# Graph layer with neighbour quantiles: the last pair's upper tiles sorted batch by batch

## The chip, the cores and the metric

One core of a Trainium2 chip runs the whole kernel. The metric is the time of one execution on the device in microseconds (us), and less is better.

## What is computed

For each of 16 batches there are N = 1024 nodes with C = 64 features and a symmetric 0/1 adjacency. Features are normalised and passed through a relu, edges are dropped by a rule on ranks, and each node takes three weighted quantiles over the neighbours that are left, feature by feature. A two-layer network and the residual follow. The reference, cut:

```
h = relu(layernorm(x))
nb   = number of neighbours;  skip = (nb + 1) // 2 where nb > 10, else 1
rem  = neighbour & (skip > 1) & (rank % skip == skip - 1);  rem |= rem.T
nd   = (adjacency or self) without rem
s    = sort of h over the neighbours in nd, feature by feature
agg  = sum over (0.25, 0.25), (0.5, 0.5), (0.75, 0.25) of w * (s[lo] + frac * (s[hi] - s[lo]))
y    = relu((h + agg) @ W1 + b1) @ W2 + b2          # 64 -> 128 -> 64
out  = x + y * mask
```

The adjacency has a density of about 1/128, so a node has some 8 neighbours before edges are dropped.

## The kernel before

**Pairs and tiles.** The batches go in eight pairs (m = 0 to 7). For each batch `prepare` reads the adjacency, drops edges, ranks what is left and writes lists of neighbours (`idx`, L1116). Nodes are put in order of their number of neighbours and cut into 8 tiles of 128. Tiles share buffers by class, `CLASSES = (((0,), 13), ((1, 2, 3), 11), ((4, 5), 9), ((6, 7), 7))`: buffer g0 holds tile 0 with 13 slots, g1 tiles 1 to 3, g4 tiles 4 and 5, g6 tiles 6 and 7. Tiles 0 to 3 are the lower half, 4 to 7 the upper. A slot holds one neighbour's 64 features for both batches of the pair.

**Gathers.** An indirect DMA on POOL's queue (`fetch`, L1250) brings 128 rows of 64 features into one slot. A pair takes 126 of them, in the order of the classes, and in each class first all slots of the pair's first batch and then all of its second; the upper classes take 30 and 18.

**Sorting.** `aggregate` (L1329) runs a network of minima and maxima on DVE over the slots of a buffer (`sort`, L1270; operations L1285, L1288, L1289), multiplies the sorted rows by weights (L1296), and PE adds them into `acc` (L1298, with a 128x128 identity in float32). A tiny DVE write, `pause` (L1268), is what PE waits for. Some nodes with many neighbours keep slots in another tile's buffer as guests: ACT copies them across (L1352), and only then may DVE overwrite their old place (L1355). `terms` splits `acc` into three bf16 parts in `o` (ACT L1312, PE L1314). A half works on both batches at once, so its instructions are twice as wide as one batch needs. In the last pair (batches 14 and 15) the lower half goes first, then the upper.

**Back to node order.** `mlp` multiplies `o` by one-hot matrices `at_p` (L1373) to bring the rows back to node order: 8 matmuls `high` (L1392) and 8 `low` (L1397) for each half of a batch's nodes, one of each for every tile. ACT copies both out (L1404, L1406), two float32 products with W1 follow (L1410, L1411), a relu (L1414), the second layer (L1424, L1428), the mask `mask2` (L1432), the residual (L1433), and a DMA of the batch to `out` (L1419).

**Rows apart.** The 32 nodes of a batch with most neighbours are sorted elsewhere, in groups of eight batches (`gg`, `aggregate_group`). Their finished rows are put into `out` by an indirect DMA on POOL's queue (`scatter`, L1498, two for a group), after the batch's own rows: `mask2` zeroes their contribution there. The last group holds batches 8 to 15, so it is scattered at the end of the program. After that come the flag that tells whether a node had too many neighbours (`worst`, L1593, L1594), its load by all engines (L1686), and a branch (L1687) over a dense version that is not taken here.

**What sets the order.** `arrange` collects the whole program and puts the instructions of every engine in a fixed order, with a cost per instruction that it reckons itself (`Step.cost`). An engine then works through its list in that order; an instruction that has to wait holds up all behind it.

Of the kernel before, what the change touches and what calls it, by code (L numbers as in the profile page):

```python
# [600 lines left out]
class Step:  # L601
# [11 lines left out]
    def cost(self):  # L613
        sides = self.writes + self.reads
        most = max([u.count for u in sides] or [1])
        if self.engine == "PE":
            n, lines = self.writes[0].count, self.writes[0].lines
            if any(u.size == 4 for u in self.reads):
                busy = 223 if n <= 64 else max(428, n / 0.6)
            else:  # L620
                busy = max(25, n / 2.4 + 3)
# [127 lines left out]
def list_layer(  # L749
# [262 lines left out]
    def order(b):  # L1012
# [30 lines left out]
        nc.vector.scalar_tensor_tensor(mask2[:, b], place_f, float(FEW), mask[:, b], OP.is_ge, OP.mult)  # L1043
# [227 lines left out]
    def sort(lines, plan, first, coef, acc):  # L1271

        size = lines.shape[2]
# [19 lines left out]
        for n in taken:  # L1293
            now, ends = ends[:n], ends[n:]
            v = at(now[0], now[1] - now[0] if n > 1 else 0, n).rearrange("p s (k c) -> p s k c", c=C)
# [33 lines left out]
    def aggregate(m, o):  # L1329


        last = m == pairs - 1
        coef = coefs[m]
        for half in (0, 1) if last else (1, 0):
            acc = psum.tile([P, 4, 2, C], F32, name="acc", tag="agg", bufs=2)
            parts = CLASSES[2 * half:2 * half + 2][::1 if last else -1]
            for tiles, slots in parts:
                lo, n = tiles[0], len(tiles)
                nc.tensor.matmul(
                    acc[:, lo - 4 * half:lo - 4 * half + n], ident32, gathered[m, tiles][:, slots - 1],  # L1340
                    start=((tiles, slots) == parts[0]), stop=False, skip_group_check=True,
                )
            line = {}
            for tiles, slots in parts:
                for k in tiles:
                    for s, slot in enumerate(PLANS[slots][1]):
                        line[k, s] = gathered[m, tiles][:, slot, k - tiles[0]]
                        if s >= FULL[k] and (k, s) not in HOSTS:
                            nc.vector.memset(line[k, s], BIG)
            for host, guest, first, stop in GUESTS:  # L1350
                if host in line:
                    nc.scalar.copy(line[guest][first:stop], line[host][first:stop])  # L1352
            for host, lo, hi in BARE:
                if host in line:
                    nc.vector.memset(line[host][lo:hi], BIG)  # L1355
            for tiles, slots in parts:
                lo, n = tiles[0], len(tiles)
                g = gathered.pop((m, tiles))
                plan = PLANS[slots]
                yield from sort(  # L1360
                    g.rearrange("p s n h c -> p s (n h c)"), plan, window(tiles, slots)[0],
                    lambda s, many: coef[:, s:s + many, lo:lo + n].rearrange("p s n h -> p s (n h)"),
                    acc[:, lo - 4 * half:lo - 4 * half + n],
                )
            if half and not last:
                fetch(m + 1, CLASSES[2:])
            terms(acc, [o[:, 4 * half:4 * half + 4, :, C * n:C * n + C] for n in range(3)])
# [14 lines left out]
    def mlp(b, o):  # L1382

        res = wk.tile([P, NT, C], F32, name="y")
        nc.sync.dma_start(out=res, in_=x[b].rearrange("(t p) c -> p t c", p=P))
        for n in range(2):
            if (b, n) not in placed:
                yield from one_hot(b, n)
            at = placed.pop((b, n))
            high = psum.tile([P, HALF], F32, name="high", tag="agg", bufs=2)  # L1390
            settle([
                nc.tensor.matmul(high, o[:, t, 0:2 * C], at[:, t], start=(t == 0), stop=(t == NT - 1))  # L1392
                for t in range(NT)
# [378 lines left out]
```

## Time and profile before

| | |
|---|---|
| median of 15 runs | 1582.53 us (1577.84 to 1585.58) |
| profiled execution | 1581.2 us |
| its span, from the first to the last instruction | 1579.5 us |
| mean granted TensorE clock in it | 0.851 |
| first gather, last upper gather on POOL | 273.57 us, 1516.84 us |
| span's end less the last DVE operation on `y` | 16.1 us |

The span is the length of the profiled execution as the trace shows it; 1.7 us of the execution lie outside. Times in the rows below count from the start of the span. A row of the timeline gives the start, the duration, the engine, the line, the operation, output and inputs, and in brackets how long the engine was idle before and what ended that. A row of the groups gives the count, the busy time and the mean duration in ns, then the idle time before. DVE, ACT, PE, POOL and SP are the five engines; a letter q behind one means its instruction queue, where waits and branches stand.

### The profile page before, as it was taken

How to read it: one execution, taken by the hardware profiler on the slowest of the kernel's cores; microseconds unless marked ns; L12 is line 12 of the kernel's file. 1: busy time of each engine (PE TensorE's matmuls, PEld its weight loads, DVE VectorE, ACT ScalarE, POOL GpSimd, SP SyncE). 2: the span in 40 equal slices, each digit the busy share in tenths (PEclk: the TensorE clock that was granted, in tenths of full speed). 3: DMA queues.
4: the chain of work that ended last, by engine and by line, in shares of the span. 5: the costliest groups of instructions: out<-in, count | busy, mean ns of one | idle time of the engine just before them, and what ended most of it. 6: DMA issues, size and time to landing. Idle time of an engine off the chain costs nothing.

```text
span 1579.5 us, 25586 instructions
## 1 busy us (share of the span) xinstructions
PE 1059.6 (67%) x8371; PEld 657.9 (42%) x8385; DVE 1192.8 (76%) x3723; ACT 915.5 (58%) x2496; POOL 1140.4 (72%) x1051
## 2 busy tenths in 40 slices
PE   6777867889878887888569745488768712602235
PEld 3445444555554454545345424354435402301122
DVE  4625499956997789879884898977988997697660
ACT  6998886987958694978276931856826200200001
POOL 3177776777777777777777777777777777777730
PEclk9989979999998999899689976899979955955568
DMA  6353442442523252325232422323211211211100
GB/s 208 113 164 93 116 110 64 113 126 60 156 57 112 59 144 63 105 60 145 50 83 67 125 64 46 85 73 65 77 26 26 50 27 25 54 25 23 21 11 18
DMA packets 128481, 122.71 MB, mean 78 GB/s; under 512 B 94514, under 2 KB 95026, under 8 KB 128338
## 3 DMA queue, kind: packets, MB, share of 16 engines
q1 hardware_dynamic: 94994, 86.77, 19.4%
q0 software_dynamic: 33344, 34.21, 10.9%
q8 instruction: 68, 1.11, 0.3%
q14 instruction: 75, 0.61, 0.1%
HBM read 110.10 MB, written 9.07 MB: 75 GB/s over the span
## 4 chain that ended last, share of the span: by engine, by line
POOL 30%; ACT 22%; DVE 15%; issue 13%; PE 13%; DMA 6%; POOLq 0%; DVEq 0%; SPq 0%; ACTq 0%
POOL g L1250 28%; PE codeP L1072 5%; DMA g<-gtab,idx 4%; DVE g L1288 4%; ACT dist L978 4%; ACT sg L891 3%; DVE g L1289 3%; ACT kept L1001 3%; ACT ne L911 3%; ACT waste L1170 2%; ACT waste L1165 1%; ACT xt L1178 1%; PE tp L898 1%; POOL gg L1455 1%; PE rk L968 1%
## 5 line engine op out<-in xcount | busy, mean ns | idle before, releaser
L1250 POOL DMA_INDIRECT g<-gtab,idx x1008 | 1092.5, 1084 | 359.1 <-issue 289.8
L1288 DVE TENSOR_TENSOR g<-g 128x512 f32<-128x512 f32 (+3 forms) x408 | 281.6, 704 | 43.6 <-DMA g<-gtab,idx 26.7
L1289 DVE TENSOR_TENSOR g<-g 128x512 f32<-128x512 f32 (+3 forms) x408 | 282.4, 705 | 10.7 <-DMA gg<-g 8.1
L1298 PE MATMUL acc<-g,kf 128*128 128x256 f32 (+2 forms) x448 | 142.3, 459 | 182.1 <-DVE pause L1268 109.2
L1072 PE MATMUL codeP<-pack,perm 128*128 128x332 bf16 x1024 | 182.2, 318 | 21.9 <-DVE perm L1047 21.4
L978 ACT ACTIVATE dist<-rk,bias 128x512 f16<-128x512 f32 x256 | 167.3, 701 | 25.1 <-DVE bias L953 11.8
L1298 PEld LDWEIGHTS acc<-g,kf 128*128 128x128 f32 x448 | 89.4, 231 | 208.7 <-DVE pause L1268 115.5
L968 PE MATMUL rk<-kb,cnt 128*128 128x512 bf16 x256 | 109.0, 426 | 73.4 <-ACT dist L978 67.3
L1001 ACT ACTIVATE kept<-kp 128x512 fp8e4<-128x512 f32 x248 | 149.3, 620 | 13.6 <-PE kp L996 11.8
L898 PE MATMUL tp<-kb,sg 128*128 128x128 bf16 x1024 | 106.3, 241 | 72.1 <-ACT sg L891 54.7
L911 ACT ACTIVATE ne<-tp 128x512 fp8e4<-128x512 f32 x248 | 138.8, 612 | 19.4 <-PE tp L904 10.9
L973 PEld LDWEIGHTS <-ne 128*128 128x128 fp8e4 x1024 | 87.2, 106 | 129.1 <-issue 104.4
L891 ACT ACTIVATE sg<-at 128x1024 bf16<-128x1024 f32 x121 | 127.0, 1081 | 3.9 <-DMA at<-in_adj_dram 3.8
L1072 PEld LDWEIGHTS <-perm 128*128 128x128 bf16 x1024 | 91.9, 100 | 86.0 <-DVE perm L1047 45.6
L898 PEld LDWEIGHTS <-sg 128*128 128x128 bf16 x1024 | 80.3, 109 | 94.0 <-ACT sg L891 63.0
L973 PE MATMUL rk<-kw,ne 128*128 128x128 fp8e5 x1024 | 114.3, 237 | 0.0
L979 DVE TENSOR_SCALAR rem<-dist,half 128x1024 bf16<-128x1024 f16 x128 | 64.7, 505 | 57.2 <-ACT dist L978 56.4
L996 PE MATMUL kp<-kw,rem 128*128 128x128 fp8e5 x1024 | 99.1, 218 | 0.0
L991 PE MATMUL kp<-ne,kw 128*128 128x512 fp8e4 x256 | 97.8, 382 | 0.1
L992 PE MATMUL kp<-rem,kw 128*128 128x512 bf16 x256 | 96.9, 379 | 0.0
L1373 DVE TENSOR_SCALAR at_p<-iota,node 128x512 bf16<-128x512 f16 x256 | 83.3, 373 | 7.0 <-PE low L1397 7.0
L1077 ACT CAST st<-codeP 128x4 bf16<-128x4 f32 x128 | 21.2, 165 | 113.5 <-PE codeP L1072 113.4
(178 smaller groups left out, 2052.9 us busy)
## 6 DMA issues: line engine op xcount, KB each, us to landing
at<-in_adj_dram SPq DMA_DIRECT2D x122, 512.0 KB
g<-gtab,idx POOLq DMA_INDIRECT x1008
xt<-in_x_dram SPq DMA_DIRECT2D x16, 256.0 KB
y<-in_x_dram SPq DMA_DIRECT2D x16, 256.0 KB
gtab<-xt SPq DMA_DIRECT2D x16, 256.0 KB
out_dram<-y SPq DMA_DIRECT2D x16, 256.0 KB
spare<-in_adj_dram SPq DMA_DIRECT2D x6, 512.0 KB
gg<-g SPq DMA_DIRECT2D x32, 48.0 KB
```

Source lines behind the costliest of these rows:

```text
L891: nc.scalar.activation(sg, at, AF.Sign)
L898: run.append(nc.tensor.matmul(tp[:, s], sg[:, m * P:(m + 1) * P], ident16, start=(s == 0), stop=(s == 3 and t // 4 != n), skip_group_check ...
L911: nc.scalar.activation(to, tp, AF.Relu, saturate=False)
L968: run = [nc.tensor.matmul(rk, cnt[:, ts], blocks[:, 4 * n:4 * n + 4, None].to_broadcast([P, 4, P]), start=True, stop=False, skip_group_che ...
L973: run.append(nc.tensor.matmul(rk[:, s * P:(s + 1) * P], ne[:, 4 * n + s, ts], upper, start=False, stop=(s == 3), skip_group_check=True,))
L978: nc.scalar.activation(dist[:, n * HALF:(n + 1) * HALF], rk, AF.Abs, bias=bias[:, t:t + 1])
L1001: nc.scalar.activation(kept[:, 4 * n:4 * n + 4], kp, AF.Relu, saturate=False)
L1072: run.append(nc.tensor.matmul(flat, perm[:, t, k * P:(k + 1) * P], pack[:, t], start=False, stop=(t == NT - 1), skip_group_check=True,))
L1250: return nc.gpsimd.indirect_dma_start(out=gathered[m, tiles][:, slot, k - lo, h], out_offset=None, in_=tables[2 * m + h][0], in_offset=bas ...
L1288: nc.vector.tensor_tensor(at(f, df, n), pa, pb, one)
L1289: ins = nc.vector.tensor_tensor(pa if back else pb, pa, pb, other)
L1298: nc.tensor.matmul(acc, ident32, lines[:, s], start=False, stop=(s == now[-1] and not ends), skip_group_check=True)
```

## The change

It has seven parts.

1. The planner's cost of a PE matmul on 4-byte data is `60 + n` for fewer than 512 columns, and 850 from there, where it was 223 up to 64 columns and then the larger of 428 and n/0.6. `arrange` then orders instructions differently in the whole program, from about row 437 of DVE's list on.
2. In the last pair the upper classes are fetched batch by batch: g4 and g6 of batch 14, then g4 and g6 of batch 15.
3. `aggregate` runs the last pair's upper half for batch 14 and then for batch 15, each with instructions half as wide.
4. Ahead of each of these two, `between` builds the batch's one-hot matrices and starts `high` and `low` with the lower four tiles (`sums`). Behind each, `mlp` adds only the upper four tiles.
5. In these two batches `low` is added to the copy of `high` by DVE (L1444), so that one product with W1 (L1448) is left of two; the product with the second bias is issued ahead; `out` is written in halves of 128 KB (L1468).
6. The rows apart of batches 14 and 15 are not scattered. `bring_back` picks them out of the group's sums with four small identity matmuls, two ACT copies, three ACT casts and two DVE subtractions (L1575), and writes them as bf16 parts into tile 0 of `o`; `mask2` of these batches is the plain mask. The last group's scatter is cut to 96 of its 128 rows and stands right behind `aggregate_group`.
7. `worst` and the flag are computed ahead of the last pair's results.

POOL's list, from the last pair's gathers of tiles 1 to 3 (g_16544) to the branch at the end; g_16715 is g4, g_16891 or g_16769 is g6. Before:

```order
L1250 DMA g_16544<-gtab,idx 128x64 x54
L1250 DMA g_16715<-gtab,idx 128x64 x30
L1250 DMA g_16891<-gtab,idx 128x64 x18
L1498 DMA out_dram<-gx,gto 16384x64 x2
L1686 TENSOR_LOAD flag
L1687 COMPARE_AND_BRANCH
```

Now:

```order
L1253 DMA g_16544<-gtab,idx 128x64 x54
L1253 DMA g_16715<-gtab,idx 128x64 x15
L1253 DMA g_16769<-gtab,idx 128x64 x9
L1253 DMA g_16715<-gtab,idx 128x64 x15
L1253 DMA g_16769<-gtab,idx 128x64 x9
L1580 DMA out_dram<-gx,gto 16384x64 x2
L1772 TENSOR_LOAD flag
L1773 COMPARE_AND_BRANCH
```

The 24 gathers of batch 14 now stand ahead of the 24 of batch 15. The scatters wait for the gathers ahead of them on the queue and for `out` of batches 12 and 13, no longer for batches 14 and 15.

DVE's list at the end of the program, from the last weighting of sorted rows (g6) to the flag. Before:

```order
L1296 TENSOR_TENSOR g6_16891<-g6_16891,coef_15426 128x3x256
L1268 MEMSET pause_127 128x1
L1432 TENSOR_TENSOR yp_17518<-yp_17518,mask2_120 128x256
L1433 TENSOR_TENSOR y_17489<-y_17489,yp_17518 128x256
L1432 TENSOR_TENSOR yp_17553<-yp_17553,mask2_120 128x256
L1433 TENSOR_TENSOR y_17489<-y_17489,yp_17553 128x256
L1432 TENSOR_TENSOR yp_17591<-yp_17591,mask2_120 128x256
L1433 TENSOR_TENSOR y_17562<-y_17562,yp_17591 128x256
L1432 TENSOR_TENSOR yp_17626<-yp_17626,mask2_120 128x256
L1433 TENSOR_TENSOR y_17562<-y_17562,yp_17626 128x256
```

Now:

```order
L1300 TENSOR_TENSOR g6_16769<-g6_16769,coef_15426 128x3x2x64 x2
L1271 MEMSET pause_127 128x1
L1444 TENSOR_TENSOR highs_17710<-highs_17710,low_17579 128x512
L1444 TENSOR_TENSOR highs_17726<-highs_17726,low_17589 128x512
L1491 TENSOR_TENSOR yp_17713<-yp_17713,mask2_120 128x256
L1492 TENSOR_TENSOR y_17692<-y_17692,yp_17713 128x256
L1491 TENSOR_TENSOR yp_17729<-yp_17729,mask2_120 128x256
L1492 TENSOR_TENSOR y_17692<-y_17692,yp_17729 128x256
```

Four rounds of mask and residual stood behind the last sorted row, one for each half of each batch; now two do, those of batch 15, and batch 14's stand among batch 15's sort.

ACT's list in the last pair, from the rows apart (`few`) to the last terms of batch 14's upper half (acc_17375; acc_17220 is the lower half). Copies from g4 to g6 are the guests, first those of batch 14 and then those of batch 15:

```order
L1569 COPY few_17367<-back_17362 32x128
L1570 COPY few_17367<-back_17362 16x128
L1364 COPY g6_16769<-g4_16715 64x64
L1364 COPY g6_16769<-g4_16715 32x64
L1316 CAST o_17019<-acc_17220 128x8x64 x2
L1573 CAST o_17019<-few_17367 32x2x64
L1364 COPY g6_16769<-g4_16715 64x64
L1316 CAST o_17019<-acc_17220 128x8x64
L1573 CAST o_17019<-few_17367 32x2x64 x2
L1364 COPY g6_16769<-g4_16715 32x64
L1316 CAST o_17019<-acc_17375 128x4x64 x3
```

Batch 15's first guest copy stands between the first and the second cast of `few`, and DVE's two subtractions on `few` stand between operations of batch 14's sort.

The diff, cut:

```
-                busy = 223 if n <= 64 else max(428, n / 0.6)
+                busy = 60 + n if n < 512 else 850
...
-    def aggregate(m, o):
+    def aggregate(m, o, between=None):
...
+            for sides in ((0, 1), (1, 2)) if last and half else ((0, 2),):
+                hs, one = slice(*sides), sides[0] if last and half else None
...
+                if one is not None:
+                    yield from between(one, False)
...
+                            line[k, s] = gathered[m, tiles][:, slot, k - tiles[0], hs]
...
+                    else:
+                        lines, weigh = g[:, :, :, one], partial(
+                            lambda s, many, lo, n, h: coef[:, s:s + many, lo:lo + n, h], lo=lo, n=n, h=one
+                        )
...
+                    for h in ((0, 1),) if m < pairs - 2 else ((0,), (1,)):
+                        fetch(m + 1, CLASSES[2:], halves=h)
...
+                if last and not half:
+                    bring_back(m, o)
+                if one is not None:
+                    yield from between(one, True)
...
+    def sums(o, at, n, some, tiles=None, late=False):
...
+        if begun:
+            begun = [sums(o, placed[b, n], n, range(NT // 2, NT), begun[n]) for n in range(2)]
...
+                nc.scalar.copy(highs, high)
+                nc.vector.tensor_tensor(highs, highs, low, OP.add)
+                run = bias(4, *(("misc", 1), ("agg", 2))[n])
+                hp = psum.tile([P, HALF], F32, name="hp", tag="code", bufs=2)
+                nc.tensor.matmul(hp, w1, highs, start=True, stop=True)
...
+    def bring_back(m, o):
...
+                run.append(nc.tensor.matmul(
+                    back[:SLICE + SLICE * q, q, h], ident32[:, lo - SLICE * q:lo + SLICE], sums[:, C * q:C * q + C],
+                    start=not run, stop=(len(run) == 3), skip_group_check=True,
+                ))
...
+        nc.scalar.copy(few, back[:, 1])
+        nc.scalar.copy(few[:SLICE], back[:SLICE, 0])
+        for n in range(3):
+            to = o[:FEW, 0, :, C * n:C * n + C]
+            nc.scalar.copy(to, few)
+            if n < 2:
+                nc.vector.tensor_tensor(few, few, to, OP.subtract)
...
+            def between(h, done):
+                b = 2 * m + h
+                if not done:
+                    for n in range(2):
+                        yield from one_hot(b, n, *((("at_p", 1), ("ne", 2)), (("ne", 2), ("wide", 1)))[h][n])
+                    begun[h] = [sums(o[:, :, h], placed[b, n], n, range(NT // 2), late=True) for n in range(2)]
+                else:
+                    yield from mlp(b, o[:, :, h], begun[h])
...
             yield from aggregate_group(grp - 1)
+            scatter(grp - 1, P - 2 * SLICE)
+            yield from aggregate(m, o, between)
...
-    for grp in range(B // GROUP):
-        if ("out", grp) in gathered:
-            scatter(grp)
```

207 lines of the change are left out of this document (122 added, 85 removed).

## The prediction

> **What bounds the kernel now.** I read the page's head first, then the shares of the chain that ended last, then POOL's timeline.
>
> ```profile
> PE 1059.6 (67%) x8371; PEld 657.9 (42%) x8385; DVE 1192.8 (76%) x3723; ACT 915.5 (58%) x2496; POOL 1140.4 (72%) x1051
> POOL 30%; ACT 22%; DVE 15%; issue 13%; PE 13%; DMA 6%; POOLq 0%; DVEq 0%; SPq 0%; ACTq 0%
> L1250 POOL DMA_INDIRECT g<-gtab,idx x1008 | 1092.5, 1084 | 359.1 <-issue 289.8
> ```
>
> No engine is full, and the chain passes through all of them. POOL's gathers tell more: 1008 of them, and nearly all of the idle time ahead of them is "issue", in which POOL waits for nobody.
>
> ```profile
> 273.57 0.94 POOL L1250 DMA_INDIRECT g<-gtab,idx  x1 [6.22 <-DVE idx L1116]
> 392.49 0.26 DVE L1116 SCALAR_TENSOR_TENSOR idx<-bit,low 128x104 int32<-128x104 f32 x1
> 412.52 1.57 POOL L1250 DMA_INDIRECT g<-gtab,idx  x1 [0.31 <-PE rk L973]
> 1444.42 0.94 POOL L1250 DMA_INDIRECT g<-gtab,idx  x1 [0.31 <-issue]
> 1516.84 0.94 POOL L1250 DMA_INDIRECT g<-gtab,idx  x1 [0.30 <-issue]
> ```
>
> At 273.57 POOL waits for the last time for a list of neighbours. At 412.52, where a later pair's list is first needed, that list has been there for 20 us (392.49 + 0.26), and POOL pauses 0.31 as ever. From 273.57 to 1517.78 it issues 858 gathers at 1.45 us each, 1.08 of issue and the rest a fixed gap. So the program is three stretches: up to 273.57, a gather-bound one to 1517.8, and a tail of 61.7 us. The change can gain in the tail only; elsewhere it can lose, where it makes POOL wait, or gain or lose by the gathers' length. The tail in windows, cut at the first upper gather, the last gather's landing, the first weighted sum that nothing sorts behind, and the end of DVE's last residual (columns: the window, its length, busy PE, PEld, DVE, ACT, POOL, then the granted clock):
>
> ```profile
> 1444.42:1519.50 75.08, 15.66 (x33) 8.55 (x34) 52.61 (x103) 2.35 (x5) 59.04 (x48) 0.55 0.11 22
> 1519.50:1531.90 12.40, 0.00 (x0) 0.00 (x0) 11.92 (x28) 0.00 (x0) 0.00 (x0) 0.59 0.00 0
> 1531.90:1563.40 31.50, 28.18 (x128) 15.53 (x130) 4.29 (x10) 9.20 (x15) 0.00 (x0) 0.95 0.04 9
> 1563.40:1579.50 16.10, 0.19 (x2) 0.11 (x2) 0.15 (x1) 0.00 (x0) 1.99 (x2) 0.58 0.12 26
> ```
>
> While the upper gathers come, POOL and DVE work; then DVE alone, then PE, then nearly nothing. The change aims at the last two windows.
>
> **Step 1: end of the upper sort.** The rows of the sort by width, with the places where it waits:
>
> ```profile
> L1288 DVE TENSOR_TENSOR g<-g 128x768 f32<-128x768 f32 x16 | 15.3, 956 | 10.7 <-issue 9.0 <-DMA g<-gtab,idx 1.5
> L1288 DVE TENSOR_TENSOR g<-g 128x512 f32<-128x512 f32 x17 | 11.8, 695 | 8.5 <-DMA g<-gtab,idx 6.6 <-issue 1.6
> L1288 DVE TENSOR_TENSOR g<-g 128x384 f32<-128x384 f32 x5 | 2.8, 562 | 0.0
> L1288 DVE TENSOR_TENSOR g<-g 128x256 f32<-128x256 f32 x7 | 3.0, 425 | 0.0
> L1285 DVE TENSOR_TENSOR g<-g 128x128 f32<-128x128 f32 x3 | 0.9, 297 | 0.0
> 1391.41 0.43 DVE L1288 TENSOR_TENSOR g<-g 128x256 f32<-128x256 f32 x1
> 1391.74 0.57 DVE L1289 TENSOR_TENSOR gg<-gg 128x384 f32<-128x384 f32 x1
> 1481.61 0.94 POOL L1250 DMA_INDIRECT g<-gtab,idx  x1 [0.30 <-issue]
> 1484.67 0.29 ACT L1352 COPY g<-g 64x128 f32<-64x128 f32 x1 [42.90 <-DMA g<-gtab,idx]
> 1485.05 0.17 DVE L1355 MEMSET g<- 64x128 f32 x1 [8.30 <-ACT g L1352]
> 1519.50 0.69 DVE L1288 TENSOR_TENSOR g<-g 128x512 f32<-128x512 f32 x1 [6.63 <-DMA g<-gtab,idx]
> ```
>
> Both batches together the upper sort is 34 operations of 512 columns, 10 of 256 and 4 of 768: 34 x 0.695 + 10 x 0.425 + 4 x 0.956 = 31.7 us. Batch by batch it is 68 of 256, 20 of 128 and 8 of 384: 28.9 + 5.9 + 4.5 = 39.3. So it costs 7.6 us more. Part comes back: operations on different buffers overlap (0.33 from start to start at 1391.41, against 0.43), and batch 14's g6 now stands between its g4's operations; about 50 pairs x 0.09 = 4.5.
>
> The Trainium skill, "VectorE: DVE Perf Modes", section "The TRN2 errata", speaks against this part: a fixed latency is paid for every instruction, so small tiles pay it oftener, and it advises at least 512 elements. By its formula for this operation, (N+151)/0.96, 48 more instructions cost an estimated 7.6 us. The rows 695 and 425 agree (0.27 for 256 columns leaves 0.16 fixed), and the overlapped pair shows that it is not always paid.
>
> What pays for the 7.6 are the waits of DVE before: 8.30 for the guests and 6.63 for the last gather, 15 us within 1476 to 1519.5. Batch 14's gathers are now the first 24 of 48, over by about 1481 instead of 1516, so batch 15's waiting is filled with batch 14's work. I walked DVE's new list with these durations and with gathers at their old times. It waits about 2.5 us at batch 14's first guest and 3 at the next, the latter over at about 1472. Behind that stand 15 operations of 768 left of the lower half (14.3), 1 + 8 of 384 (5.1), 66 of 256 (28.1), 20 of 128 (5.9), two `highs` of 512 (1.4) and mask, residual and `few` (2.3): 57 us, less 4.5 of overlap. The waits in it I put at 8.5: two for ACT at `few`, where ACT stands behind batch 15's guest copy, which needs a gather ending at about 1498 (2.6 and 5.0), and 0.9 at `highs`. So it ends at 1472 + 52.5 + 8.5 = 1533, against 1531.9: no gain. The bounds: waits at `few` of nothing give 1525; but no operation can stand ahead of the data of the last 9 gathers (g6 of batch 15), whose sort is some 28 half-width operations, 28 x 0.4 = 11, so not before 1519.5 + 9 = 1528.5 with overlap. Above, 5 us more waiting gives 1538. I take 1533.
>
> **Step 2: the last sum.** The rows from here to the end:
>
> ```profile
> 1531.94 4.49 PE L1298 MATMUL acc<-g,kf 128*128 128x256 f32 x12 [13.57 <-DVE pause L1268]
> 1398.68 3.63 PE L1298 MATMUL acc<-g,kf 128*128 128x128 f32 x15 [26.73 <-DVE g L1296]
> 1536.46 0.59 ACT L1312 CAST o<-acc 128x512 bf16<-128x512 f32 x1 [39.87 <-PE acc L1298]
> 1538.53 0.86 PE high L1392 x4
> 1539.39 0.98 PE low L1397 x8
> 1540.40 1.12 PE hp L1410 x2
> 1560.10 0.70 ACT h L1414
> 1561.54 0.85 PE yp L1428 x8
> 1562.47 0.45 DVE yp L1432
> 1562.94 0.43 DVE y L1433
> 1563.39 2.58 DMA out_dram<-y
> ```
>
> Twelve matmuls of 256 columns took 4.49, and end at 1536.44. Now 12 of 128 columns stand there, 0.24 each by the row at 1398.68: 2.9. The last sum ends at 1533 + 2.9 = 1535.9.
>
> **Step 3: from the last sum to the last residual.** Before: 1536.44 to 1563.37, 26.9 us: three casts, then four rounds of 5.9 (1540.40 to 1546.36 between two `hp`), PE nearly full. Now one batch is left, with half its tiles: casts and subtractions on 256 columns 2.0, `high` and `low` 0.86 + 0.49, the copy 0.55 and the new DVE addition 0.69, one `hp` pass of about 1.05, the relu 0.70, `yp` 0.85, mask and residual 0.88: 8.1, and the second half of the nodes 1.2 behind it: 9.3. The window before has a clock of 0.59 while PE idles, and PE idles less than that here but for some us; the twelve float32 sums at 0.37 each show it slow at the start. If all PE work in it, 5.1 us, ran at half speed, it is 14.4. I take 10.8, nearer to the warm rows, since the mean clock of the window from 1531.90 is 0.95.
>
> **Step 4: from the last residual to the end.** Before: 16.1 us. The chain goes through the DMA of `out`, which the scatters wait for, and through POOL's drain at the program's end:
>
> ```profile
> 1566.94 1.00 POOL L1498 DMA_INDIRECT out_dram<-gx,gto  x1 [49.15 <-DMA out_dram<-y]
> 1570.39 0.99 POOL L1498 DMA_INDIRECT out_dram<-gx,gto  x1 [2.46 <-DMA out_dram<-gx,gto]
> L1687 PEldq COMPARE_BRANCH  x1: 3675/3675/3675, 1564.6 to 1564.6; - x1
> L1687 SPq EVENT_SEMAPHORE  x8: 17/17/17, 1568.0 to 1568.6; - x8
> L1768 POOLq DRAIN  x3: 40/113/7366, 1571.3 to 1579.2; - x3
> L1768 SPq EVENT_SEMAPHORE  x14: 17/28/4583, 1568.6 to 1579.4; - x14
> ```
>
> Now the scatters stand behind the last gather, at about 1518, with `out` of batches 12 and 13 long landed, and POOL then loads the flag and reaches its drain near 1524; 7.4 of drain are over at about 1531, under the sort. What is left behind the last residual: the transfer of 2.58, beside the flag's load and PE's branch of 3.7 (0.5 + 3.7), SP's eight semaphores (0.6 + 0.4), and the closing exchange between engines (1578.7 to 1579.5, 0.8): 6.0, or 4.4 if PE's branch, which needs no residual, is over by then. POOL's drain is no cover of anything else, and SP, which waits for the `y` loads and four half transfers before its branch, holds nobody up who has work. I take 5.4. The upper bound is that with the drain at the end after all, 5.4 + 7.4 = 12.8.
>
> **What costs nothing, or an unknown.** `bring_back` (4 small matmuls, 5 ACT copies of 0.2 to 0.3, 2 DVE subtractions) lies under the gathers; its waits are in step 1. The one-hots and the lower halves' products lie there too: PE had 15.66 us busy in the 75 before 1519.50, so it has room for the 16 us that it does earlier. [...] The planner's new costs change the order in the gather-bound stretch. As long as lists come 20 us early, that moves nothing but how DVE's copies and sorts fall on gathers, and a gather alone takes 0.94 against 1.084 on average: 145 us of 1008 gathers is contention, and 3% of it, either way, is 4 us. Up to 273.57 the lists and the gathers' order stay; 0 +- 2.
>
> **Sum, against the span of 1579.5.** Sort end +1.1, last sum -1.6, step 3 -16.1, step 4 -10.7: -27.3, so 1552.2. The execution adds 1.7: 1553.9. The profiled one, 1581.2, is 1.3 under the median; so 1555.
>
> **Rivals.**
> - *The sort gets longer* (0.16). Each wait at `few`, guests and `highs` stops all that stands behind it on DVE. If ACT comes later than I walked, with g1's sums late, the sort ends at 1541 or so, and the time is 1563. For it: 8.30 us of such a wait before, for one guest copy. Against: the list has independent work between.
> - *The drain stays at the end* (0.06). If POOL's 7366 ns is paid after all engines meet and not when POOL gets there, the time is 1555 + 7.4 = 1562. For it: the row stands after the branch. Against: it began when POOL's last scatter ended (1570.39 + 0.99), so it seems to follow POOL alone.
> - *Waits by the whole buffer* (0.04), the other sign. If batch 14's sort waited for batch 15's gathers into the same g4 and g6, its first row would stand at 1519.5, with 15 operations of g1 and all the upper sort behind it: 57 us, ending at 1576.5, and steps 2 to 4 make 1576.5 + 2.9 + 10.8 + 5.4 = 1595.6, or 1598.6 in the measure. It turns the gain into a loss once DVE waits 27 us more than I walked. For it: the trace of before never shows one batch sorted while the other's gathers into its buffer still come. Against: in the new program the waits ahead of batch 14's operations count its own gathers alone.
> - *POOL waits in mid-program* (0.06). A list late by more than the 20 us of slack stops POOL, and each us counts: with 30 late it is 1565, and to cancel the gain a list would have to be late by 47 us in one pair.
> - *The change does less*: the order moves, but ACT and PE take batch 14's rounds late, behind batch 15's sort (0.04). Then two rounds come back, 1555 + 11.8 = 1567.
>
> **How the numbers follow.** The forecast has 0.64. Its own range: step 1 from 1528.5 to 1538, step 3 from 9.3 to 14.4, step 4 from 4.4 to 6, contention +-4: all at one end make 1544 and 1568, and as they are independent, 1548 to 1563. The cases at 1562 to 1567 hold 0.32 and the last sign's 0.04. The range 1545 to 1569 takes these in, with all but the ends of the forecast's bounds, and leaves out the loss and a part of the mid-program case. 0.2%, or 3.2 us, is about what a measurement of this kernel tells from no change. Faster: all but the loss and a part of the mid-program case, 0.92; same 0.02; slower 0.06.
>
> **What will show it.** Right: the last weighted sum near 1533, four halves of `out` of which two leave before 1533, POOL's scatters at about 1520 and its drain before 1535, one `hp` per half, and 5 to 6 us from the last residual to the end. Wrong: DVE waits over 10 us in total behind 1472 on `few` or guests; a gather that waits for `idx` between 400 and 1500; a mean gather beyond 1.11 us; the drain behind the last `out`.

## The result, and the profile after

The changed kernel takes 1542.85 us (median of 9 runs, 1539.12 to 1549.59) against 1583.08 for the kernel before (47 runs): a ratio of 0.9754, with an interval of 0.9739 to 0.9769, or 39 us less. The forecast was 1555, a gain of 27.3 against the span, with a range from 1545. The direction and the tail came as forecast; 10 us came from a place for which the sum had nothing and the range 4 us.

The page's head, its chain by engine and its row of gathers, for the changed kernel:

```profile
PE 1065.1 (69%) x8395; PEld 664.6 (43%) x8411; DVE 1203.3 (78%) x3799; ACT 915.1 (59%) x2504; POOL 1127.6 (73%) x1051
PE 30%; ACT 26%; DVE 17%; POOL 11%; issue 10%; DMA 4%; SPq 0%; DVEq 0%; POOLq 0%; ACTq 0%
L1253 POOL DMA_INDIRECT g<-gtab,idx x1008 | 1079.0, 1070 | 362.0 <-issue 287.7
```

Against the same rows before, DVE is busier (1203.3 against 1192.8), as forecast, and the gathers are shorter: 1070 ns against 1084, 13.5 us over all 1008. POOL's share of the chain fell from 30% to 11%, though behind 276.78 no gather waits for a list any more, so what bounds this stretch is read from POOL's timeline and not from the chain. That timeline, at the last wait for a list and at the end:

```profile
276.78 0.94 POOL L1253 DMA_INDIRECT g<-gtab,idx  x1 [8.68 <-DVE idx L1119]
1506.50 0.95 POOL L1253 DMA_INDIRECT g<-gtab,idx  x1 [0.30 <-issue]
1507.75 0.93 POOL L1580 DMA_INDIRECT out_dram<-gx,gto  x1 [0.30 <-DVE g L1292]
```

The last of these gathers ends at 1507.45, where it was 1517.78. The first starts 3.2 us later than before (273.57). And a scatter now follows the last gather at once. The tail in windows, cut at the first upper gather, the last gather's end, the last weighted row (where PE's last sums can start), the last residual and the span's end (columns as in the prediction's windows):

```profile
1436.11:1507.45 71.34, 26.81 (x92) 12.52 (x94) 57.96 (x159) 7.09 (x18) 57.02 (x48) 0.62 0.12 22
1507.45:1520.66 13.21, 7.80 (x45) 5.40 (x44) 12.17 (x48) 0.69 (x1) 1.86 (x2) 0.79 0.14 28
1520.66:1535.04 14.38, 12.28 (x51) 7.09 (x52) 3.54 (x8) 3.66 (x7) 0.00 (x0) 0.72 0.01 3
1535.04:1541.60 6.56, 0.00 (x0) 0.00 (x0) 0.00 (x1) 0.00 (x0) 0.00 (x0) 0.54 0.23 48
```

PE now works beside DVE in the second window (7.80 us, 0.00 before): these are batch 14's rounds. Single rows of the tail, on ACT, DVE and PE:

```profile
1486.09 0.58 ACT L1316 CAST o<-acc 128x512 bf16<-128x512 f32 x1 [22.93 <-PE acc L1302]
1488.07 0.24 ACT L1364 COPY g<-g 64x64 f32<-64x64 f32 x1
1488.08 0.28 DVE L1575 TENSOR_TENSOR few<-few,o 32x128 f32<-32x128 f32 x1 [3.21 <-ACT o L1573]
1520.70 2.93 PE L1302 MATMUL acc<-g,kf 128*128 128x128 f32 x12 [3.23 <-DVE g L1300]
1528.10 0.69 DVE L1444 TENSOR_TENSOR highs<-highs,low 128x512 f32<-128x512 f32 x1 [6.98 <-PE low L1423]
1534.62 0.42 DVE L1492 TENSOR_TENSOR y<-y,yp 128x256 f32<-128x256 f32 x1
```

Counted from the end of the last gather:

| | before | forecast | measured |
|---|---|---|---|
| end of the last gather | 1517.8 | 1517.8 | 1507.5 |
| to the last weighted row | 14.1 | 15.2 | 13.2 |
| last sum | 4.5 | 2.9 | 3.0 |
| to the last residual | 26.9 | 10.8 | 11.4 |
| to the end | 16.1 | 5.4 | 6.6 |
| tail | 61.7 | 34.3 | 34.2 |

That the two tails agree to 0.1 us is in part luck: the sort ended 2.0 us sooner behind the last gather than forecast, and the other three pieces took 1.9 us more.

The rows of the program's end:

```profile
L1773 SPq EVENT_SEMAPHORE  x8: 17/17/17, 1538.4 to 1539.0; - x8
L1773 PEldq COMPARE_BRANCH  x1: 3695/3695/3695, 1533.6 to 1533.6; - x1
L1854 SPq EVENT_SEMAPHORE  x14: 17/28/28, 1539.0 to 1541.5; - x14
L1854 POOLq DRAIN  x3: 40/112/7294, 1511.1 to 1541.3; - x3
```

POOL's drain of 7.3 us begins at 1511.1 and is over at 1518.4, before the sort is. PE's branch starts before the last residual and ends at 1537.3; SP's semaphores follow.

In part of the runs below the kernels took 2533 to 2735 us and the kernel before beside them 2571 to 2612; of those only what stands behind the gathers is read, and ratios to the kernel before beside them, by which the changed kernel was no gain there (1.0124, 1.0041 to 1.0206).

### The profile page after: what moved, and what is told of

The parts are those of the page before. It is cut to its first block, busy times and chain, and to the rows that moved or that the text cites. A ratio compares the mean times of both kernels' runs of the same rounds, so it can differ in the third digit from the quotient of the medians.

```text
span 1541.6 us, 25721 instructions
## 1 busy us (share of the span) xinstructions
PE 1065.1 (69%) x8395; PEld 664.6 (43%) x8411; DVE 1203.3 (78%) x3799; ACT 915.1 (59%) x2504; POOL 1127.6 (73%) x1051
## 3 DMA queue, kind: packets, MB, share of 16 engines
q1 hardware_dynamic: 95026, 86.77, 19.5%
q0 software_dynamic: 33344, 34.19, 11.2%
q8 instruction: 68, 1.11, 0.3%
## 4 chain that ended last, share of the span: by engine, by line
PE 30%; ACT 26%; DVE 17%; POOL 11%; issue 10%; DMA 4%; SPq 0%; DVEq 0%; POOLq 0%; ACTq 0%
POOL g L1253 10%; PE codeP L1075 8%; DVE g L1291 6%; PE acc L1302 5%; ACT dist L978 5%; DVE g L1292 4%; ACT sg L891 4%; ACT ne L911 3%; ACT kept L1001 3%; PE tp L898 2%; PE rk L968 2%; PE rk L973 2%; DMA g<-gtab,idx 2%; ACT waste L1168 2%; DMA xt<-in_x_dram 2%
## 5 line engine op out<-in xcount | busy, mean ns | idle before, releaser
L1253 POOL DMA_INDIRECT g<-gtab,idx x1008 | 1079.0, 1070 | 362.0 <-issue 287.7
L1291 DVE TENSOR_TENSOR g<-g 128x768 f32<-128x768 f32 (+3 forms) x428 | 284.0, 678 | 14.3 <-DMA g<-gtab,idx 12.2
L1292 DVE TENSOR_TENSOR g<-g 128x512 f32<-128x512 f32 (+3 forms) x428 | 284.4, 679 | 10.9 <-DMA gg<-g 6.9
L1302 PE MATMUL acc<-g,kf 128*128 128x128 f32 (+2 forms) x472 | 134.4, 432 | 142.5 <-DVE pause L1271 77.9
L1075 PE MATMUL codeP<-pack,perm 128*128 128x332 bf16 x1024 | 188.4, 328 | 13.1 <-DVE perm L1050 12.9
L968 PE MATMUL rk<-kb,cnt 128*128 128x512 bf16 x256 | 112.1, 438 | 95.4 <-ACT dist L978 91.6
L1302 PEld LDWEIGHTS acc<-g,kf 128*128 128x128 f32 x472 | 87.1, 224 | 167.0 <-DVE pause L1271 81.9
L898 PE MATMUL tp<-kb,sg 128*128 128x128 bf16 x1024 | 109.4, 247 | 69.5 <-ACT sg L891 53.8
L911 ACT ACTIVATE ne<-tp 128x512 fp8e4<-128x512 f32 x248 | 139.5, 613 | 15.3 <-PE tp L904 8.3
L898 PEld LDWEIGHTS <-sg 128*128 128x128 bf16 x1024 | 83.2, 112 | 91.2 <-ACT sg L891 60.8
L973 PE MATMUL rk<-kw,ne 128*128 128x128 fp8e5 x1024 | 120.0, 242 | 0.0
```

The costliest lines, as they stand in the source:

```text
L898: run.append(nc.tensor.matmul(tp[:, s], sg[:, m * P:(m + 1) * P], ident16, start=(s == 0), stop=(s == 3 and t // 4 != n), skip_group_check ...
L911: nc.scalar.activation(to, tp, AF.Relu, saturate=False)
L968: run = [nc.tensor.matmul(rk, cnt[:, ts], blocks[:, 4 * n:4 * n + 4, None].to_broadcast([P, 4, P]), start=True, stop=False, skip_group_che ...
L973: run.append(nc.tensor.matmul(rk[:, s * P:(s + 1) * P], ne[:, 4 * n + s, ts], upper, start=False, stop=(s == 3), skip_group_check=True,))
L1075: run.append(nc.tensor.matmul(flat, perm[:, t, k * P:(k + 1) * P], pack[:, t], start=False, stop=(t == NT - 1), skip_group_check=True,))
L1253: return nc.gpsimd.indirect_dma_start(out=gathered[m, tiles][:, slot, k - lo, h], out_offset=None, in_=tables[2 * m + h][0], in_offset=bas ...
```

## The experiments

**What makes a gather long.** The first question was why the 884 gathers after 273 us (858 for the pairs, 26 for the rows apart) took 14.2 us less: 952.1 instead of 966.3. I laid every gather beside the DVE operations that run as it starts. In the kernel before, on POOL and DVE:

```profile
1470.15 1.68 POOL L1250 DMA_INDIRECT g<-gtab,idx  x1 [0.30 <-issue]
1472.14 1.68 POOL L1250 DMA_INDIRECT g<-gtab,idx  x1 [0.30 <-DMA g<-gtab,idx]
1470.06 0.96 DVE L1289 TENSOR_TENSOR g<-g 128x768 f32<-128x768 f32 x1
1472.04 0.96 DVE L1289 TENSOR_TENSOR g<-g 128x768 f32<-128x768 f32 x1
```

Each gather starts 0.1 us into an operation of 768 columns, and ends 0.82 us after that operation has ended (1473.00, 1473.82). A gather alone takes 0.94. So it waited for the rest of that one operation, less 0.12. Taken as a rule (the gather waits for the rest, less 0.12, of the operation of two float32 inputs that began last, if that was at least 0.05 us before the gather), it gives 109.9 us of waiting over 381 gathers of the kernel before, where 109.3 was measured, and 99.2 against 101.6 over 388 in the changed one; 366 and 374 of these agree to 0.04 us each.

The rule leaves gathers out. Over 0.94 us each, all 884 lost 135.4 us before and 121.1 after, so 26.1 and 19.5 us are lost by gathers that it does not cover. The largest part of that, 14.5 and 12.5 us, is lost by gathers begun inside a TENSOR_SCALAR of DVE, such as this one of the kernel before (the row of DVE holds eight in a row):

```profile
313.98 1.28 POOL L1250 DMA_INDIRECT g<-gtab,idx  x1 [0.30 <-issue]
312.68 3.25 DVE L1047 TENSOR_SCALAR perm<-turned,place_f 128x1024 bf16<-128x1024 f16 x8
```

What such a gather waits for was not worked out.

A kernel of its own tests this apart from all else. It computes nothing of the reference: it runs stretches of 24 gathers, beside which DVE works on two buffers that nobody else touches, with one width in each stretch:

```
for n in range(int(52 / step) if wide else 0):
    i = n % chains
    a, b = low[i][:, :wide], high[i][:, :wide]
    if n // chains % 2:
        vector(nc.vector.tensor_tensor(b, a, b, OP.max))
    else:
        vector(nc.vector.tensor_tensor(a, a, b, OP.min))
```

A first form was to hold all widths in turn (theory A is the rule, rival C that DVE's busy share counts):

> A kernel of its own that computes nothing of the reference: seven stretches of 24 gathers (128 rows of 64 features, as the kernels issue them), beside which DVE works without a pause on minima and maxima of one width in two buffers that nobody else touches; nothing waits for anything within a stretch. Theory A (a gather that finds a float32 operation of two inputs running as it starts goes on when that one operation ends; 0.94 us plus the rest of the operation less 0.12): a mean gather of 0.94 without DVE, then 1.01 beside 128 columns, 1.06 beside 256, 1.03 beside 384, 1.15 beside 512, 1.67 beside 768, and 1.11 beside two chains of 384 in turn. Rival C (a gather is slowed by DVE's busy share): DVE is busy all the time in each, so all six are alike within 0.1, about 1.1 to 1.2.

Its operations of several widths ran mixed, and those of 512 and 768 columns behind the gathers, so it said nothing by itself (all gathers but the first took 0.94 to 1.09). In the second form DVE's order is fixed:

> The kernel of gathers beside one width, again: in the first try DVE's operations of all widths ran mixed, behind the gathers or ahead. Now every stretch holds one width (two stretches without DVE first). Theory A (a gather that finds a float32 operation running as it starts goes on when that one operation ends: 0.94 us plus the rest of it less 0.12): mean gathers 0.94 without DVE, then 1.01 beside 128 columns, 1.06 beside 256, 1.03 beside 384, 1.15 beside 512, 1.67 beside 768, and 1.11 beside two chains of 384 in turn. Rival C (DVE's busy share counts): all six alike within 0.1.

Windows of it, within the stretches without DVE, beside 128, 256, 384, 512 and 768 columns and two chains of 384 (columns: the window, its length, busy DVE, busy POOL with the count of gathers, clock, DMA share, GB/s), and one gather beside 128 columns:

```profile
36.60:68.41 31.81, 0.16 (x3) 22.70 (x24) 1.00 0.09 25
68.50:100.30 31.80, 18.32 (x64) 23.19 (x24) 1.00 0.09 25
133.50:163.60 30.10, 27.86 (x67) 23.34 (x22) 1.00 0.09 23
185.56:215.70 30.14, 28.48 (x51) 22.77 (x24) 1.00 0.09 25
239.19:274.00 34.81, 33.21 (x49) 27.44 (x24) 1.00 0.07 22
290.82:338.30 47.48, 45.85 (x50) 40.09 (x24) 1.00 0.06 16
342.50:376.20 33.70, 33.70 (x74) 26.31 (x24) 1.00 0.08 23
79.21 1.00 POOL L50 DMA_INDIRECT got<-in_x_dram,idx  x1 [0.30 <-issue]
```

POOL's busy time over its count is a mean gather: 0.95, 0.97 (1.00 while DVE works without a break; it paused in the second half), 1.06, 0.95, 1.14, 1.67 and 1.10. The rule gave 0.94, 1.01, 1.06, 1.03, 1.15, 1.67, 1.11. Five of the seven agree to 0.01; beside 128 and beside 384 columns the gathers took 0.04 and 0.08 less than the rule's number. DVE is busy 94 to 97% beside 384 and beside 768, and the gathers differ by 0.72 us, so rival C falls. What counts is where in an operation a gather begins. Beside 384 columns the gathers fell into step: 21 of 24 began 0.03 to 0.04 us behind an operation's start, and did not wait. Beside 768 all but the first began 0.09 to 0.10 us behind one, and waited 0.74 each.

**Part 1 alone, and all but part 1.** The edits are the one line of the planner's cost, put into the kernel before, and taken out of the changed one. The kernel before took 1581 and 1580 us beside them.

> The kernel before with part 1 alone, a third time. Where the kernel before takes about 1583: theory A 1572 to 1574, rival B 1583 +- 3, as said for the first run of it. Where it takes about 2570 again: 1.03 of the kernel before, as in the two runs of it so far.

> The changed kernel with the old cost (all parts but part 1), a fourth time. Where the kernel before takes about 1581: theory A (part 1 holds the gathers' gain, the other parts the tail's 27.6) 1553 to 1556, and the gathers' lengths over 0.94 sum to about 139 us as before. Rival B (the other parts shorten the gathers too): 1544 to 1550, with a sum of 125 to 132. Where the kernel before takes about 2570: 0.991 to 0.994 of it, as before.

Part 1 alone: 1575.6 us, 0.9968 (0.995 to 0.9985), a gain of 5, with gathers of 953.8 us after 273, a first one 5.4 us later and a tail of 61.6 us: theory A but for 2 us. All but part 1: 1549.11, 0.9813 (0.9787 to 0.9839), a gain of 30, with a tail of 35.3 us. The gathers alone in windows from the first behind the last wait to the last pair's first tile, and from there to the last gather, in the order before, all but part 1, part 1 alone, changed (columns: window, length, the pairs' gathers' busy time and count, clock, DMA share, GB/s):

```profile
273.50:1333.70 1060.20, 809.65 (x743) 0.87 0.31 77
1333.70:1517.80 184.10, 129.94 (x115) 0.64 0.15 30
275.40:1333.80 1058.40, 806.77 (x743) 0.87 0.32 78
1333.80:1512.10 178.30, 124.31 (x115) 0.68 0.17 31
278.90:1328.90 1050.00, 799.30 (x743) 0.85 0.32 78
1328.90:1511.00 182.10, 128.20 (x115) 0.63 0.16 31
276.70:1327.10 1050.40, 798.79 (x743) 0.86 0.31 78
1327.10:1507.50 180.40, 126.38 (x115) 0.66 0.16 31
```

For all but part 1 theory A's 1553 to 1556 failed and rival B's 1544 to 1550 held; its gathers lost 128.1 us over 0.94 each, within B's 125 to 132, where the kernel before has 135.4 (the expectation said 139). In the first stretch the two kernels with the new cost lose 10.4 and 10.9 us of gathers, the one without it 2.9, though DVE's order there is that of the kernel before but for a few neighbours that changed places: 2.9 is then about what two profiles of one order differ by. In the last pair all but part 1 lose 5.6 us, part 1 alone 1.7. So the new cost shortens the gathers of the first seven pairs by some 8 to 10 us, in one profile each; the first gather starts 5.4 and 3.2 us later with it, and 1.9 without it.

The rule does not tell where these 8 to 10 us come from. In the first stretch the gathers that it covers lost 87.0 us in the order before and 83.2 in all but part 1, one order, against 82.0 and 83.3 with the new cost. Those that it leaves out lost 25.9 and 28.2 with the old cost, and 20.4 and 19.1 with the new. Of these last, gathers begun inside a TENSOR_SCALAR lost 14.5 and 15.1, then 11.2 and 12.5, and gathers begun less than 0.05 us behind the start of an operation of two inputs 6.3 and 7.2, then 3.0 and 2.4. So most of this part of the gain is in waits that the rule does not describe, and what they are stays open.

In the last pair nearly all waiting is by the rule. The other parts shorten its gathers by 2 to 6 us: where the upper sort is not split, 18 and 19 gathers wait 11.3 and 12.0 us for operations of 768 columns, and where it is split, 12 and 13 wait 5.6 and 7.5. That this is the split's doing was not shown apart from the other parts.

**Operations of 768 columns cut in two.** If waits for the widest operations set the kernel's time, narrow operations should give more. The edit, in `sort`, for all pairs but the last:

```
+            cut = [slice(i, min(i + max(1, wide // size), n)) for i in range(0, n, max(1, wide // size))]
...
-                nc.vector.tensor_tensor(at(f, df, n), pa, pb, one)
+                for c in cut:
+                    nc.vector.tensor_tensor(at(f, df, n)[:, c], pa[:, c], pb[:, c], one)
...
+                        10**9 if last else 512,
```

> The changed kernel with DVE's operations of more than 512 columns cut into pieces of one slot in all pairs but the last, a third time. Where the kernel before takes about 1581: theory A (a gather waits for the end of the one operation that runs as it starts): 138 gathers wait 48.9 us for operations of 768 columns in the changed kernel; for 384 columns they wait 0.17 to 0.26 at most, and beside a chain of them in step with the gathers not at all, so 15 to 25 us are saved: 1518 to 1530. Rival C (DVE's busy share counts, and DVE is busier): 1541 to 1550. Where the kernel before takes about 2570: 1.037 of it, as before.

It took 1538.89 us, 0.9737 (0.9721 to 0.9753) of the kernel before: 2 to 3 us under the changed kernel by the ratios, whose intervals overlap. The windows as above:

```profile
277.40:1320.80 1043.40, 792.93 (x743) 0.86 0.32 79
1320.80:1501.30 180.50, 126.32 (x115) 0.67 0.17 31
```

The expected 15 to 25 us were missed; the gathers got 6 us shorter (946.2 against 952.1). By the rule's own count gathers waited 8.9 us for 768 columns instead of 53.0, but 231 of them now met an operation of 384, where 93 did, and waited 44.1 us instead of 16.2; other widths took 4 more. About as many gathers were caught as before (398 against 388), those beside 384 for half as long each (0.19 against 0.36). The rule's sum for them, 87.1 us, stands beside 90.5 measured, so the rule stands and the estimate failed: it took the catches at 768 away and did not count those that cutting makes. It has the lowest time measured here, by less than can be told.

**The tail's two gains.** Part 6 undone (the scatter of all 128 rows behind the last output, no `bring_back`), and parts 2 to 5 undone (no split: `for sides in ((0, 2),):`, four full rounds behind it):

> The changed kernel with part 6 undone (rows apart scattered behind the last output, no bring_back, mask2 as before). By the forecast's step 4 the end behind the last residual is 16.1 us again instead of 6.5, and nothing else moves: a tail of 34 + 9.6 = 43.7 us behind the last gather's issue. Rival: DVE's wait at few (3.2 us) also cost the sort, which then ends 3 us earlier: 40.5 us.

> The changed kernel with parts 2 to 5 undone (upper half of the last pair for both batches at once, four full rounds behind it), the rows apart still brought back and scattered early. By the forecast's steps: sort end 14 us behind the last gather's issue, last sum 4.5, four rounds 26.9, end 6.5: a tail of 52 us. Rival: the early scatter and the waits at few cost DVE in the tail, so it is 55 us or more; or the drain's 7.4 us were hidden by the split sort only, then 59.

> The changed kernel with part 6 undone, a second time. Where the kernel before takes about 1581: the end behind the last residual is 15 to 16 us instead of 6.6, all else stays: 8 to 10 us over the changed kernel, 1549 to 1552 (0.980 to 0.982 of the kernel before). Rival (DVE's wait at few also cost the sort): 1546 to 1549.

> The changed kernel with parts 2 to 5 undone, a second time. Where the kernel before takes about 1581: the tail behind the last gather's issue is 52 us instead of 34. Theory A (the split also took 6 us from the last pair's gathers, since DVE's operations of 768 columns then stand among narrow ones): 18 + 4 to 6 us over the changed kernel, 1563 to 1566. Rival (the last pair's gathers are short by chance of the order): 18 us over it, 1558 to 1561.

Both took 2588 to 2656 us in all of their runs. There the sort ends 165 to 170 us behind the last gather in either kernel (172.3 in the changed kernel beside them, where its own tail was expected to be 34), so the expected tails of 43.7 and 52 us can't be read. From the last sum on they can: there the changed kernel has 11.8 us to the last residual and 7.5 from there, and the kernel before with part 1 alone 26.8 and 16.1, near to the 11.4, 6.6, 26.9 and 16.1 of the table above. Windows from the last sum to the last residual and on to the end, for part 6 undone, its drain on POOL, and for parts 2 to 5 undone:

```profile
2561.27:2570.93 9.66, 7.81 (x41) 4.15 (x39) 3.09 (x6) 3.67 (x7) 0.00 (x0) 0.96 0.02 4
2570.93:2586.10 15.17, 0.00 (x0) 0.00 (x0) 0.00 (x0) 0.00 (x0) 2.00 (x2) 0.54 0.12 25
L1849 POOLq DRAIN  x3: 40/113/7387, 2577.9 to 2585.8; - x3
2620.39:2647.20 26.81, 23.74 (x119) 12.05 (x117) 3.38 (x8) 9.18 (x15) 0.00 (x0) 1.00 0.06 11
2647.20:2654.40 7.20, 0.00 (x0) 0.00 (x0) 0.04 (x1) 0.00 (x0) 0.00 (x0) 0.68 0.22 46
```

Without part 6 the end is 15.2 us again and POOL's drain its largest piece; without parts 2 to 5 the four rounds are 26.8 again and the end stays short, 7.2. So part 6 takes 8 to 9 us off the end and parts 2 to 5 take 15 off the rounds, and each does so without the other. The second runs of both gave 15.3 and 26.8 with 7.2. But without part 6 the last residual also comes 2 us sooner behind the last sum (9.7 and 9.5 against 11.8), and the sort ends 6 to 7 us sooner behind the last gather (166.0 and 165.5 against 172.3): counted from the last gather, the kernel without part 6 takes 193.3 and 192.8 us and the changed one 193.2. What part 6 is worth as a whole is therefore not shown. (As a whole the two took 1.0152 and 1.0213 of the kernel before, then 1.0151 and 1.0178.) Whether DVE's wait at `few` costs the sort anything at the time of the other runs stays open.

**The runs at 2533 to 2735 us.** Part 1 alone, all but part 1, the cut operations, and another cost (`busy = 300` for all widths) in the kernel before were first run there:

> The kernel before with part 1 alone (the planner's cost of 4-byte matmuls). Theory A: the time that the forecast missed lies in the gathers, which the new order of DVE's list shortens, since a gather waits for the DVE operation that runs as it starts. Then this kernel gains about 10 us (1572 to 1574), the gathers after 273 us sum to about 951 us instead of 966, the first of them starts about 3 us later, and the tail behind the last gather stays at 62 us. Rival B: the gathers got shorter by the other parts (the fetch by batch, the mask's copies, the earlier flag). Then this kernel takes 1583 +- 3 and the sum stays near 966.

> The changed kernel with the planner's old cost (all parts but part 1). Theory A: the tail's gain alone, 27.6 us: 1555.5 +- 3, gathers sum to about 966 us, and the tail behind the last gather is 34 us. Rival B: 1543 +- 3, with the gathers near 951.

> The changed kernel with DVE's sorting operations of more than 512 columns cut in pieces of one slot (768 to 2 x 384) in all pairs but the last. Theory A (a gather waits until the running DVE operation ends, so the wait is by the operation's length): the 159 gathers that start under a 768-column operation wait 0.316 on average; under 384 columns it is 0.13 to 0.18, so the gathers lose 20 to 30 us in sum and the time is 1515 to 1525, though DVE's busy time rises by 30 to 45 us. Rival C (a gather is slowed by DVE's busy share, not by the length of one operation): DVE is busier, the gathers' sum stays or rises, and the time is 1543 to 1550.

> The kernel before with another planner's cost for 4-byte matmuls, 300 for all widths. Theory A: the order's effect is a matter of where DVE's operations fall on the gathers, so any other order moves the gathers' sum by some us either way, and the time follows the sum and the first gather's start within 2 us; 1583 +- 12. Rival D: the new cost gains because it is nearer to what the matmuls take (0.24 for 128 columns, 0.37 for 256, 0.86 for 512), so one that is wrong at 512 gives 1583 or more.

They took 1.0302 (1.0264 to 1.0339), 0.9903 (0.9868 to 0.9937), 1.0367 (1.034 to 1.0394) and 1.0419 (1.0383 to 1.0456) of the kernel before beside them. The repeats came out there too:

> The kernel before with part 1 alone, again, since the chip of the first call ran every kernel a thousand us slower, with stalls of 20 to 50 us in which PE gets no instructions. Theory A (the missed gain lies in gathers that the new order shortens): on a chip where the kernel before takes about 1583 this gains about 10 us (1572 to 1574), the gathers after 273 us sum to about 951 us instead of 966, the first of them starts about 3 us later, and the tail behind the last gather stays at 62 us. Rival B (the gathers got shorter by the other parts): 1583 +- 3 and a sum near 966.

> The changed kernel with the planner's old cost, again on another chip. Theory A: the tail's gain alone, 27.6 us: 1555.5 +- 3, gathers sum to about 966 us, and the tail behind the last gather is 34 us. Rival B: 1543 +- 3, with the gathers near 951.

> The changed kernel with the old cost (all parts but part 1), a third time. Where the kernel before takes about 1581: theory A (part 1 holds the gathers' gain, the other parts the tail's 27.6) 1553 to 1556, and the gathers' lengths over 0.94 sum to about 139 us as before. Rival B (the other parts shorten the gathers too): 1544 to 1550, with a sum of 125 to 132. Where the kernel before takes about 2570: 0.991 of it, as twice before.

> The changed kernel with DVE's operations of more than 512 columns cut into pieces of one slot in all pairs but the last, a second time. Where the kernel before takes about 1581: theory A: the gathers that start under 768 columns lose 0.354 on average now (138 of them, 48.9 us); under 384 they lose 0.17 to 0.26, so 15 to 25 us are saved: 1518 to 1530. Rival C (DVE's busy share counts, and DVE is busier): 1541 to 1550. Where the kernel before takes about 2570: 1.037 of it, as before.

Part 1 alone took 2664.88 us against 2571.47 (no interval, since its times scattered from 2612 to 2671), all but part 1 took 0.9918 (0.9882 to 0.9954) and 0.9941 (0.9907 to 0.9975), the cut ones 1.0385 (1.0337 to 1.0433). A row of DVE in part 1 alone shows what differs:

```profile
151.81 0.17 DVE L949 TENSOR_SCALAR sk<-nb 128x8 int32<-128x8 f32 x1 [67.94 <-remote]
```

Its data was ready at 118.4, and POOL gathered without a pause until 147. POOL has no part in the chain that ended last in this run, and 34% of that chain is "another core or an unknown queue". Gathers are not the bound there, so these times answer neither theory. The changed kernel, expected at about 1.02 there, took 1.0124:

> The changed kernel itself beside the kernel before in one call, to hold against the kernel with the old cost. The tail behind the issue of the last gather is 34 us, as in its first profile, on any chip. Theory A (part 1 acts through the order of DVE's list in the gathers' stretch): against the kernel before it is at 0.9754 where that takes 1583; where stalls in the gathers' stretch dominate, the order decides there too, and this kernel and the one with the old cost (0.990) differ by what part 1 does alone (1.03), so about 1.02.

Every kernel with another cost lost there, and the one with the old cost and the tail's parts gained 0.6 to 1%. Why engines start so long after their data in those runs was not tried; the cost of 300 was run there alone, so how far any other order would move the gathers is open.

## Why the prediction was right or wrong

- **What bounds the kernel: right.** POOL's gathers to the end of their stretch, then the tail: the last gather ended 10.3 us sooner, and the rest of the gain, some 27.5 us, is the tail's.
- **Step 1, end of the sort: right to 2 us** (15.2 us behind the last gather forecast, 13.2 measured), though not wait by wait: 3.42 and 2.32 us at the guests, where 2.5 and 3 stood, 1.90 at `highs`, where 0.9 stood, and 3.21 once at `few`, where 2.6 and 5.0 stood. The wait at `few` also had another reason: batch 15's guest copy went through beside it at 1488.07, and ACT was late because the lower half's sums came at 1486.09.
- **Steps 2 and 3: right** (3.0 for 2.9, 11.4 for 10.8). The granted clock from the last weighted row to the last residual was 0.72, nearer to the bound of half speed than I took.
- **Step 4: right in mechanism**, the drain is hidden; 6.6 where 5.4 stood, a little beyond the 6.0 of its own range.
- **"145 us of 1008 gathers is contention, and 3% of it, either way, is 4 us": this step failed.** The mechanism was named, that a new order moves how DVE's operations fall on the gathers; the term was mis-sized. The contention fell by 10.9 us in the first seven pairs and 3.6 in the last, a tenth of it, and the 3% had no row behind it. "Up to 273.57 ... 0 +- 2" was off by 3.2 the other way. With both, the last gather ended 10.3 us sooner, and the span of 1541.6 lies 10.6 below the sum's 1552.2. A row that speaks of it was quoted (the gather of 1.57 us at 412.52), and those of 1.68 us beside operations of 768 columns were at hand. By the rule 153 gathers waited 62.0 us for operations of 768 columns, 0.40 each, and 149 waited 53.0 in the changed kernel; those that the rule leaves out lost 26.1, then 19.5. By the runs with and without part 1, the new cost took 8 to 10 us and the other parts 2 to 6. Two profiles of one order alone differ by 2.9 us, so 4 us either way was hardly more than that. Why the new order spares just these gathers stays open.
- The Trainium skill, "SBUF — State Buffer", section "Who interferes with whom", says that a DVE instruction with two SBUF inputs contends with a GpSimd instruction that reads SBUF, and that the order of issue decides who waits. The gathers alone agree: beside 768 columns those that began 0.09 us or more behind an operation's start waited 0.73 us on average, and beside 384 those that began 0.03 to 0.04 us behind one did not wait. In the kernel before 28 of 42 gathers that began less than 0.05 us behind such a start did not wait either, and 14 did. The forecast left that page out.

## What to carry to other kernels

Where one engine's long queue of indirect transfers sets the time, lay its single instructions beside what runs on the other engines as each begins: a mean can hide a wait that follows a rule, and the rule shows how much waiting there is to move. A change of a scheduler's costs is a change of that whole overlay. Its effect needs a range worked out from single waits, and one wider than what two profiles of one order differ by. Taking the widest operations away need not take the waits away, since more gathers then meet the narrower ones. A tail can be summed row by row; here each piece came within 2 us. Give each piece of it (drain, branch, scatter) to the engine that pays, and ask if it can pay early.

## What the runs showed of the hardware

A gather's mean length does not simply grow with the width of the operations beside it: 1.06 us beside 256 columns, 0.95 beside 384, 1.14 beside 512, 1.67 beside 768. Gathers and operations fall into step, 1.98 us for two operations of 768 columns and one gather.
